# A postnorm attention and FFN layer on one core: the last tile's normed rows turned by VectorE and DMAs instead of TensorE

## The chip, the core and the metric

The kernel runs on one core of a Trainium2 chip. The core has five engines with queues of their own: TensorE (PE in the profile, its weight loads PEld), VectorE (DVE), ScalarE (ACT), GpSimd (POOL) and SyncE (SP, which only issues DMAs here). They share the on-chip memory SBUF; TensorE writes its results to PSUM. The metric is the time of one execution on the device, in microseconds (us).

## What is computed

`x` holds 4 sequences of 512 rows of 1024 numbers, in 32-bit floats. The layer is

```python
q, k, v = x @ w_q.T, x @ w_k.T, x @ w_v.T        # 16 heads of 64
q, k = rope(q), rope(k)
attn = softmax(where(causal, q @ k.T, -1e9) / sqrt(64))
x = layernorm(x + (attn @ v) @ w_out.T)
x = layernorm(x + x @ (weight_int8 * scales[:, None]).T)
```

The second product, the FFN, has an int8 weight of 1024x1024 with one scale for each output.

## The kernel before

**Precision by digits.** TensorE takes its operands in a short float format (`FR`). A 32-bit operand is split into a high digit (ACT rounds a copy) and a low digit (DVE subtracts the high digit from the number), and products are made from digits. In the FFN the weight is int8 and needs one digit, so each FFN product has two parts, `hi` and `lo` (`ffn`, line 667 on). For the products with `w_q`, `w_k`, `w_v` and `w_out` both operands are split in three tiles each, high, low and a difference; those of the weights are `WD[0]` to `WD[2]`, each of 128x1024 numbers.

**Stages.** First come the units of attention (a sequence and a pair of heads each), up to about 740 us. Then come 16 tiles of 128 rows each, `t` from 0 to 15, in one loop, `for t in range(NT_ROWS)`. For a tile there are: the output product of the attention (`out_half`, line 199, two halves of 512 columns with 24 matmuls of 512 columns each), the residual and the first layer norm (`norm`), the turning of the normed rows (`transpose_x1`), the FFN product (`ffn`, line 676, two halves of 16 matmuls), and behind it the scales, the residual and the second norm. `x_sb[t]` is a tile's row buffer through all of this. In the loop the digits of tile `t`'s attention output lie in `WD[t % 3]`.

**Why rows are turned.** TensorE sums over the partitions (the 128 rows of SBUF). The output product leaves a tile with its rows on the partitions, and the FFN needs the 1024 columns there, as 8 blocks of 128. `transpose_x1` has two ways to do that:

- Tiles 0, 1 and 15: eight TensorE transposes of 128x128 into PSUM (line 647), and for each half of the columns a copy by ACT (line 649, the high digit) and a subtraction by DVE (line 650, the low digit).
- Tiles 2 to 14: DVE turns each 32x32 block (line 653, into the one buffer `blocks`), four DMAs on SP's queue carry the four quarters of the partitions to a DRAM tile `turned_x` (line 658), four more bring them back in the wanted order (line 661), into the tile that becomes the low digit. Then ACT copies the high digit (line 664) and DVE subtracts (line 665), in one piece of 128x1024 each. A load of quarter `a` reads what the store of quarter `a` wrote, and each load brings a part of every one of the 8 blocks.

Tiles 0 to 13 and 15 have their digits in the buffers `x1hi` and `x1lo`, of which there is one pair. Tile 14's lie in `WD[1]` (`WD[t % 3]` at `t` = 13), so that its loads need not wait for tile 13's product.

**Order.** TensorE's order is written out by hand (`manual_schedule`). In the loop's last three rounds it is: round 13: first half of tile 15's output product, its second half, (tile 14's turning, which gives TensorE nothing to do), tile 13's FFN product; round 14: tile 15's transposes, tile 14's FFN product; round 15: tile 15's FFN product. The orders on DVE, ACT, SP and POOL are made at build time by a planner, which takes what it reckons ready and prefers what stands earlier in the program; at run time each engine keeps to its order and waits in it. PSUM for the FFN has two buffers of 512 columns (`ps_f`), drained by DVE (lines 684 to 686: times scale, plus residual, statistics). POOL's queue carries the finished tiles to the output, SP's and ACT's queues the two halves of the last one.

Of the kernel before, what the change touches and what calls it, by code (L numbers as in the profile page):

```python
# [16 lines left out]
ALU = mybir.AluOpType  # L17
# [21 lines left out]
def attention_ffn_kernel(  # L39
# [18 lines left out]
    nc = tc.nc  # L58
# [38 lines left out]
    NT_ROWS = B * NI  # L97
# [4 lines left out]
    def norm(r, name, stats=None):  # L102

        if stats is None:
            stats = stp.tile([P, 2, 6], FP, tag="stats", name=f"stats_{name}")
            for n in range(2):
                nc.vector.bn_stats(stats[:, n, :], r[:, ts(n, 512)])
        mean, rstd = moments(name, stats)
        nc.vector.tensor_scalar(r, r, mean, rstd, ALU.subtract, ALU.mult)

    def moments(name, stats):
        mv = stp.tile([P, 2], FP, tag="mv", name=f"mv_{name}")
        nc.vector.bn_aggr(mv, stats)
        rstd = stp.tile([P, 1], FP, tag="rstd", name=f"rstd_{name}")
        nc.scalar.activation(rstd, mv[:, 1:2], AF.Sqrt, bias=eps_sb)
        nc.vector.reciprocal(rstd, rstd)
        return mv[:, 0:1], rstd
# [22 lines left out]
    def digits(name, width):  # L140
        pool = ctx.enter_context(tc.tile_pool(name=name, bufs=1, side=RIGHT_SIDE))
        return [pool.tile([P, NC, width], FR, name=f"{name}_{n}") for n in "hld"]
# [3 lines left out]
    WD = [digits(f"w{k}", P) for k in (2, 1, 0)][::-1]  # L146
# [36 lines left out]
    def load_ao(t, tile=None):  # L183

        tile = staged["w", t % 3] = stage(f"sa_{t}", [P, NC, P]) if tile is None else tile
        nc.sync.dma_start(out=tile, in_=ao[t // NI][:, :, ts(t % NI, P)])

    def load_row(t, queue=nc.sync):
        x_sb[t] = row_tiles[t % 4]
        queue.dma_start(out=x_sb[t], in_=x[ts(t, P), :])  # L190

    def out_product(t, half, n, pool, tag):

        w, r = XD[half], WD[t % 3]
        if n in (0, 2 * NC):
            oprod[n > 0] = pool.tile([P, 512], FP, tag=tag, name=f"y_{t}_{half}_{n}")
        ps = oprod[n >= 2 * NC]
        c, part = (n // 2, n % 2) if n < 2 * NC else (n - 2 * NC, 2)
        nc.tensor.matmul(  # L199
            ps,  # L200
            lhsT=r[part][:, c, :],
            rhs=w[part][:, c, :],
            start=n in (0, 2 * NC),
            stop=n in (2 * NC - 1, NT - 1),
        )
        if n in (2 * NC - 1, NT - 1):
            o = x_sb[t][:, ts(half, 512)]
            nc.vector.scalar_tensor_tensor(o, ps, 1.0 + X12 if n < NT - 1 else -X12, o, op0=MUL, op1=ADD)  # L208
            if half and n == NT - 1:
                norm(x_sb[t], f"a{t}")  # L210

    def high_w(k):
        t = staged["w", k]
        nc.scalar.activation(WD[k][0], t, AF.Copy, scale=LESS)
        nc.scalar.activation(t, t, AF.Copy, scale=1.0 / X12)
# [9 lines left out]
    def split_w(k):  # L225
        low_w(k)
        diff_w(k)
# [399 lines left out]
    with tc.tile_pool(name="row", bufs=1) as rowp, tc.tile_pool(name="sum", bufs=2) as sump, tc.tile_pool(  # L627
        name="ps_x", bufs=2, space=PSUM
    ) as ps_x, tc.tile_pool(name="ps_f", bufs=2, space=PSUM) as ps_f, tc.tile_pool(
        name="ps_o", bufs=2, space=PSUM  # L630
    ) as ps_o:
        x1T = {}

        turned_x = [tc.dram_tile([R, Q, R, NC * Q], FP, name=f"turned_x{n}") for n in range(2)]

        def transpose_x1(t, digits=None):


            if digits is None:
                digits = [rowp.tile([P, NC, P], FR, tag=f"x1{n}", name=f"x1{n}_{t}") for n in ("hi", "lo")]  # L640
            hi, lo = x1T[t] = digits[:2]
            if t in (0, 1, NT_ROWS - 1):

                for n in range(2):
                    ps = ps_x.tile([P, 4, P], FP, tag="xT", name=f"xT_{t}_{n}")
                    for c in range(4):
                        nc.tensor.transpose(ps[:, c, :], x_sb[t][:, ts(4 * n + c, P)], ident)
                    cs = slice(4 * n, 4 * n + 4)
                    nc.scalar.copy(hi[:, cs, :], ps)
                    nc.vector.tensor_tensor(lo[:, cs, :], ps, hi[:, cs, :], ALU.subtract)  # L650
                return
            blocks = rowp.tile([P, R, NC * Q], FP, tag="blocks", name=f"blocks_{t}")
            nc.vector.transpose(
                blocks.rearrange("p r (c s) -> p r c s", s=Q), x_sb[t].rearrange("p (c r s) -> p r c s", r=R, s=Q)
            )
            rows = turned_x[t % 2]
            for a in range(R):
                nc.sync.dma_start(out=rows[:, :, a, :].rearrange("r n w -> n r w"), in_=blocks[ts(a, Q)])
            x1 = lo.bitcast(FP)
            for a in range(R):  # L660
                nc.sync.dma_start(
                    out=x1[:, :, ts(a, Q)], in_=rows[:, :, a, :].rearrange("r n (c s) -> (r n) c s", s=Q)
                )
            nc.scalar.copy(hi, x1)
            nc.vector.tensor_tensor(lo, x1, hi, ALU.subtract)

        def ffn(t, last=False):
            hi, lo = x1T.pop(t)
            r = x_sb.pop(t)
            stats = stp.tile([P, 2, 6], FP, tag="stats", name=f"stats_f{t}")  # L670
            for n in range(2):
                o = ts(n, 512)
                ps = ps_f.tile([P, 512], FP, tag="f", name=f"f_{t}_{n}")
                for c in range(NC):
                    for part in (hi, lo):
                        nc.tensor.matmul(  # L676
                            ps,
                            lhsT=part[:, c, :],
                            rhs=wfv[:, c, o],
                            start=(c == 0 and part is hi),  # L680
                            stop=(c == NC - 1 and part is lo),
                        )
                f = sump.tile([P, 512], FP, tag="sum", name=f"fs_{t}_{n}")
                nc.vector.tensor_mul(f, ps, sc32[:, o])
                nc.vector.tensor_add(r[:, o], f, r[:, o])
                nc.vector.bn_stats(stats[:, n, :], r[:, o])
            if not last:
                norm(r, f"f{t}", stats)
                nc.gpsimd.dma_start(out=out[ts(t, P), :], in_=r)
                return  # L690
            mean, rstd = moments(f"f{t}", stats)
            for n, queue in enumerate((nc.sync, nc.scalar)):
                o = ts(n, 512)
                nc.vector.tensor_scalar(r[:, o], r[:, o], mean, rstd, ALU.subtract, ALU.mult)
                queue.dma_start(out=out[ts(t, P), o], in_=r[:, o])

        def out_half(t, half):
            for n in range(NT):
                out_product(t, half, n, *((pjp, "pj") if half else (ps_o, "o")))

        with tc.manual_schedule(engines={mybir.EngineType.PE}):
            for t in range(NT_ROWS):
                early = t + 2
                if 1 < t < NT_ROWS - 2:
                    out_half(early, 0)
                if t + 3 < NT_ROWS:
                    if t:
                        load_row(t + 3)
                    load_ao(t + 3, raw_ao)
                    high_w(t % 3)  # L710
                    split_w(t % 3)
                if t == 0:
                    out_half(1, 1)
                    transpose_x1(0)
                    out_half(2, 1)
                    out_half(3, 0)
                elif early < NT_ROWS:
                    transpose_x1(t)
                    out_half(early, 1)
                if t == NT_ROWS - 3:  # L720

                    transpose_x1(t + 1, WD[t % 3])
                if t == NT_ROWS - 2:
                    transpose_x1(t + 1)
                ffn(t, t == NT_ROWS - 1)


# [44 lines left out]
```

## Time and profile before

| | us |
|---|---|
| median of 3 runs (lowest to highest) | 1020.71 (1020.62 to 1022.29) |
| profiled execution | 1022.38 |
| its span, first to last instruction | 1020.6 |
| mean granted clock of TensorE | 0.995 of full |

| engine | busy us | share | instructions |
|---|---|---|---|
| PE (matmul) | 1000.3 | 98% | 4628 |
| PEld (weight load) | 744.0 | 73% | 4628 |
| DVE | 853.1 | 84% | 1246 |
| ACT | 388.3 | 38% | 841 |
| POOL | 204.1 | 20% | 283 |

The profile is of one execution. Its times are counted from the first instruction. A row of a timeline gives start, length, engine, line of the program, operation, output `<-` inputs with their shapes, how many, and in brackets the idle time of that engine ahead of it and what ended that. A row of the chain of waits gives start, length and the work that the end of the run was waiting for in that stretch. SPq, DVEq and the like are the queue of an engine issuing or waiting, not computing. "us to landing" of a DMA runs from its issue to the arrival of its data. Tiles appear under the names of their buffers: the row buffers are `row`, `cos_sb` and `sin_sb`, and digits that lie in a weight's place are `w_h` and `w_l`.

### The profile page before, as it was taken

Reading aid. Unit: us, or ns where it says so; the run is one execution under the profiler, and the core shown is the slowest. Engines: PE = TensorE matmul, PEld = TensorE weight load, DVE = VectorE, ACT = ScalarE, POOL = GpSimd, SP = SyncE. Lnnn points to the kernel's source line nnn. Section 1 sums busy time; section 2 is a strip of 40 time slices with the busy share of each in tenths; the row PEclk is TensorE's granted clock in tenths of the full one; section 3 lists DMA queues with packets and bytes.
Section 4 is the critical chain, followed back from the end, with each engine's and each line's share of the span. In section 5 each row is a group of like instructions: output and inputs, shape, how many; then the busy total and the mean of one; then the engine's idle time right before and its main releaser. Section 6 shows DMA issues by size and latency. Waiting matters only on the chain.

```text
span 1020.6 us, 13749 instructions
## 1 busy us (share of the span) xinstructions
PE 1000.3 (98%) x4628; PEld 744.0 (73%) x4628; DVE 853.1 (84%) x1246; ACT 388.3 (38%) x841; POOL 204.1 (20%) x283
## 2 busy tenths in 40 slices
PE   9999999999999999999999999998899999999997
PEld 4667777777777667777777777775588888888885
DVE  5998888888888999788898888888898877878776
ACT  4524444354544435445344453444332122121110
POOL 0122332222322322332223322231300000000000
PEclk9999999999999999999999999999999999999999
DMA  7576676867768786676867758688645465563541
GB/s 288 168 234 210 212 233 190 263 210 217 223 196 262 249 244 225 195 253 190 253 218 201 247 175 270 215 252 275 206 135 154 124 160 145 125 169 103 144 104 62
DMA packets 264022, 204.09 MB, mean 200 GB/s; under 512 B 147600, under 2 KB 220304, under 8 KB 263824
## 3 DMA queue, kind: packets, MB, share of 16 engines
q1 hardware_dynamic: 256176, 184.60, 60.4%
q10 hardware_dynamic: 5616, 10.75, 2.8%
q0 software_dynamic: 2160, 7.87, 1.9%
q8 instruction: 37, 0.61, 0.3%
q14 instruction: 33, 0.27, 0.1%
HBM read 112.46 MB, written 73.92 MB: 183 GB/s over the span
## 4 chain that ended last, share of the span: by engine, by line
PE 88%; DVE 5%; issue 3%; DMA 2%; ACT 1%; POOL 1%; SPq 0%; ACTq 0%; DVEq 0%; POOLq 0%
PE p L276 44%; PE y L199 17%; PE f L676 11%; PE s L409 7%; PE o L490 6%; PE pw L261 3%; DVE pr L463 1%; DVE x_d L177 1%; POOL pr L458 1%; DVE x_l L173 1%; DVE nmx L430 0%; DMA rot<-raw 0%; DVE raw L318 0%; DMA sx<-in_xT 0%; DVE w_l L219 0%
## 5 line engine op out<-in xcount | busy, mean ns | idle before, releaser
L458 POOL TENSOR_SCALAR pr<-pr,rden 128x128 f32<-128x128 f32 (+3 forms) x256 | 192.9, 772 | 528.6 <-DVE rden L452 464.7
L276 PE MATMUL p<-x_h,w_h 128*128 128x512 f32 x736 | 290.2, 394 | 0.0
L276 PE MATMUL p<-x_l,w_l 128*128 128x512 f32 x736 | 286.8, 390 | 0.0
L276 PE MATMUL p<-x_d,w_d 128*128 128x512 f32 x736 | 190.9, 395 | 2.8 <-DVE v L318 2.4
L444 ACT ACTIVATE pr<-s,nmx 128x128 f32<-128x128 f32 (+3 forms) x256 | 131.4, 531 | 115.5 <-DVE nmx L430 110.2
L276 PEld LDWEIGHTS p<-x_h,w_h 128*128 128x128 f32 x736 | 138.1, 188 | 50.4 <-issue 22.0
L276 PEld LDWEIGHTS p<-x_d,w_d 128*128 128x128 f32 x736 | 135.5, 188 | 36.1 <-issue 5.1
L276 PEld LDWEIGHTS p<-x_l,w_l 128*128 128x128 f32 x736 | 138.2, 188 | 28.1
L295 ACT ACTIVATE tA<-p 128x512 f32<-128x512 f32 x92 | 55.1, 599 | 223.4 <-PE p L276 218.4
L463 DVE STREAM_TRANSPOSE pr<-pr 128x768 f32<-128x768 f32 (+1 forms) x96 | 99.6, 1056 | 24.4 <-POOL pr L458 22.5
L199 PE MATMUL y<-x_h,w_h 128*128 128x512 f32 x256 | 101.7, 397 | 4.4 <-ACT tA L295 3.9
L430 DVE TENSOR_REDUCE nmx<-s 128x2 f32<-128x256 f32 (+3 forms) x128 | 102.0, 820 | 4.2 <-PE s L419 1.1
L199 PE MATMUL y<-x_l,w_l 128*128 128x512 f32 x256 | 101.4, 396 | 2.2 <-DVE x_l L173 2.1
L676 PE MATMUL f<-wf,x1hi 128*128 128x512 f32 x240 | 93.4, 389 | 0.0
L676 PE MATMUL f<-wf,x1lo 128*128 128x512 f32 x240 | 93.4, 389 | 0.0
L409 PE MATMUL s<-qk 64*128 64x384 f32 (+3 forms) x512 | 80.2, 446 | 1.0 <-DVE qk L242 1.0
L490 PE MATMUL o<-prT,va 128*64 128x256 f32 (+3 forms) x512 | 76.0, 439 | 0.5 <-ACT pr L444 0.5
L223 DVE TENSOR_TENSOR w_d<-w_h,w_l 128x1024 fp32r<-128x1024 f32 x60 | 74.5, 1241 | 1.5
L318 DVE SCALAR_TENSOR_TENSOR raw<-p,tA 128x512 f32<-128x512 f32 x61 | 41.8, 685 | 38.4 <-PE p L276 38.4
L490 PEld LDWEIGHTS o<-prT,va 128*64 128x64 f32 x512 | 33.9, 136 | 46.2 <-issue 40.0
L199 PE MATMUL y<-x_d,w_d 128*128 128x512 f32 x256 | 64.9, 396 | 0.5 <-DVE sin_sb L208 0.5
L199 PEld LDWEIGHTS y<-x_h,w_h 128*128 128x128 f32 x256 | 48.6, 190 | 15.7 <-ACT tA L295 4.3
(112 smaller groups left out, 1157.4 us busy)
## 6 DMA issues: line engine op xcount, KB each, us to landing
turned<-pr SPq DMA_DIRECT2D x64, 384.0 KB, 3.6
rot<-raw SPq DMA_DIRECT2D x128, 128.0 KB, 2.7
turned<-pr SPq DMA_DIRECT2D x32, 512.0 KB, 4.5
prT<-turned SPq DMA_DIRECT2D x32, 512.0 KB, 5.3
prT<-turned SPq DMA_DIRECT2D x32, 384.0 KB, 4.0
turned_v<-v SPq DMA_DIRECT2D x32, 256.0 KB, 4.7
va<-turned_v SPq DMA_DIRECT2D x128, 64.0 KB, 2.8
prT<-turned SPq DMA_DIRECT2D x32, 256.0 KB, 3.3
```

What stands on the lines that cost most here:

```text
L199: nc.tensor.matmul(ps, lhsT=r[part][:, c, :], rhs=w[part][:, c, :], start=n in (0, 2 * NC), stop=n in (2 * NC - 1, NT - 1),)
L223: nc.vector.tensor_tensor(d, h, l, SUB)
L276: nc.tensor.matmul(ps, lhsT=w[part][:, c, :], rhs=r[part][:, c, :], start=n in (0, 2 * NC), stop=n in (2 * NC - 1, NT - 1),)
L295: nc.scalar.activation(prod["tA"], ps, AF.Copy, scale=1.0 + X12)
L318: nc.vector.scalar_tensor_tensor(raw_tile(u, k), ps, -X12, prod["tA"], op0=MUL, op1=ADD)
L409: nc.tensor.matmul(ps[:, j, at : at + n], lhsT=t[rows, 0, ts(i, P)], rhs=keys[rows, :, : (i + 1) * Q], start=True, stop=u not in BUSY,)
L430: nc.vector.tensor_reduce(nmx[:, 2 * i : 2 * i + 2], ps[:, :, at : at + n], AX.X, ALU.max, negate=True)
L444: nc.scalar.activation(pr[:, :, at // P : at // P + i + 1, j, :], ps[:, j, at : at + n].rearrange("p (r k s) -> p r k s", r=R, s=Q), AF.Ex ...
L458: nc.gpsimd.tensor_scalar(p, p, rden[:, m : m + 1], 1.0, ALU.mult, ALU.mult)
L463: nc.vector.transpose(t, t)
L490: nc.tensor.matmul(ps[j * D : (j + 1) * D, kb * P :], lhsT=v[:, kb, 2 * j : 2 * j + 2, :].rearrange("p a s -> p (a s)"), rhs=t[:, :, 4 * k ...
L676: nc.tensor.matmul(ps, lhsT=part[:, c, :], rhs=wfv[:, c, o], start=(c == 0 and part is hi), stop=(c == NC - 1 and part is lo),)
```

## The change

Tile 15 no longer takes the way over TensorE. It is turned as tiles 2 to 14 are, and its `transpose_x1` moves from round 14 into round 13, behind tile 14's and ahead of tile 13's FFN product. Its digits lie in `WD[(13 + 1) % 3]`, that is `WD[2]`, where tile 14's attention output was. For this tile alone copy and subtraction are made in two halves of four column blocks each; all other tiles keep one piece.

```diff
-            if t in (0, 1, NT_ROWS - 1):
+            if t < 2:
...
-            nc.scalar.copy(hi, x1)
-            nc.vector.tensor_tensor(lo, x1, hi, ALU.subtract)
+            for cs in (slice(0, 4), slice(4, 8)) if t == NT_ROWS - 1 else (slice(0, 8),):
+                nc.scalar.copy(hi[:, cs, :], x1[:, cs, :])
+                nc.vector.tensor_tensor(lo[:, cs, :], x1[:, cs, :], hi[:, cs, :], ALU.subtract)
...
                 if t == NT_ROWS - 3:
 
                     transpose_x1(t + 1, WD[t % 3])
-                if t == NT_ROWS - 2:
-                    transpose_x1(t + 1)
+                    transpose_x1(t + 2, WD[(t + 1) % 3])
                 ffn(t, t == NT_ROWS - 1)
```

## The prediction

> **What bounds the kernel now.** I read the page first (TensorE, PE, busy 98% of the span), then the chain of waits over the last 120 us, then each engine's timeline over the last 45 us, then the landing times of the two DMA lines. All times below are us on the axis of the kernel before. The chain:
>
> ```profile
> 979.24 10.92 PE y L199 x48
> 990.16 7.27 PE f L676 x32
> 997.43 0.87 PE xT L647 x8
> 998.30 14.75 PE f L676 x64
> ...
> 1016.00 0.03 issue
> 1016.02 0.55 DVE row L694
> 1016.57 0.46 DVEq L768
> ```
>
> From 900 to 1013 the path is PE alone, without a gap. The eight transposes of the last tile (xT, L647) lie on it, between the second product of tile 13 and that of tile 14. Behind 1013 stands a tail of VectorE (DVE), a square root and the last DMA, which the change does not touch. So PE work taken away here shortens the run one for one, as long as PE is given no wait in its place. The exact starts:
>
> ```profile
> 997.26 1.04 PE L647 MATMUL xT<-ident,row 128*128 128x128 f32 x8
> 998.05 0.48 PE L676 MATMUL f<-wf,w_h 128*128 128x512 f32 x1
> 998.37 0.40 PE L676 MATMUL f<-wf,w_l 128*128 128x512 f32 x1
> ```
>
> The transposes hold PE from 997.26 to 998.05, 0.79. The first product after them stands 0.32 before its follower, others 0.23. The two products of 32 matmuls on both sides, one window each (length, then PE and weight-load busy time with counts, granted clock, DMA share, GB/s):
>
> ```profile
> 990.00:997.26 7.26, 7.26 (x32) 5.82 (x31) 1.00 0.00 0
> 998.05:1005.61 7.56, 7.55 (x33) 6.11 (x33) 1.00 0.18 69
> ```
>
> Tile 14's product takes 0.30 longer than tile 13's at the same granted clock, 1.00.
>
> **What the change removes: PE's transposes.** Surely 0.79. With them goes the stretched first product, 0.32 - 0.23 = 0.09. The other 0.21 of the 0.30 runs through all of tile 14's product. It may be an after-effect of the transposes (then it goes) or belong to digits that lie in a weight's buffers (then it stays, and tile 15's product, now fed from such buffers too, gains up to 0.30 as well). So PE's saving lies between 0.79 - 0.30 = 0.49 and 0.79 + 0.30 = 1.09. The nearest row speaks against the buffers: the products of line 199 read such buffers as weights, and 16 of them from 984.56 to 988.18 are 0.226 apart. I take 0.79 + 0.09 + half of 0.21 = 1.0. Tile 15's product, at 1005.61 before, could then start at 1004.6 (1004.8 if only the 0.79 is gained).
>
> Also removed are two ACT copies (L649) and two DVE subtractions (L650) out of PSUM. Their successors have the same number and width (128x512), so on these engines they are moved, not saved.
>
> **What it adds: a trip for the last tile.** It is one 128x1024 DVE block transpose (L653), four DMAs to DRAM (L658) and four back (L661) on SP's queue, then copy and subtraction in halves. DVE around the place:
>
> ```profile
> 974.23 0.81 DVE L109 TENSOR_SCALAR row<-row,mv_a,rstd_a 128x1024 f32<-128x1024 f32 x1
> 975.08 1.25 DVE L653 STREAM_TRANSPOSE blocks<-row 128x1024 f32<-128x1024 f32 x1
> 976.25 0.65 DVE L684 TENSOR_TENSOR fs<-f,sc 128x512 f32<-128x512 f32 x1
> ...
> 993.19 0.81 DVE L109 TENSOR_SCALAR row<-row,mv_a,rstd_a 128x1024 f32<-128x1024 f32 x1
> 993.92 0.68 DVE L684 TENSOR_TENSOR fs<-f,sc 128x512 f32<-128x512 f32 x1
> ...
> 997.46 0.69 DVE L684 TENSOR_TENSOR fs<-f,sc 128x512 f32<-128x512 f32 x1 [1.41 <-PE f L676]
> ```
>
> Tile 14's block transpose followed its norm after 0.85 and stood ahead of the product's drain (L684). The code puts tile 15's likewise ahead of tile 13's product, so it should start at 993.19 + 0.85 and end at F = 995.3. It pushes tile 13's first drain back by 1.17, and the 1.41 of idle time before 997.46 hides that; without this cover, DVE would be 1.17 late to the second drain, done with that PSUM buffer by 999.3, and PE wants it for tile 14's second half at 1000.9.
>
> SP's queue and the landings (first line 658, out; then line 661, in):
>
> ```profile
> 976.35 0.95 SPq L658 DMA_DIRECT2D turned_x<-blocks  x2
> 979.27 2.61 SPq L661 DMA_DIRECT2D x1lo<-turned_x  x4
> 981.92 1.43 SPq L658 DMA_DIRECT2D turned_x<-blocks  x2
> 983.40 4.16 SPq L661 DMA_DIRECT2D w_l<-turned_x  x4
> 1016.60 0.36 SPq L695 DMA_DIRECT2D out<-row  x1
> ...
> DMA to landing us min/median/max: 2.0/3.0/4.7
> ...
> DMA to landing us min/median/max: 3.1/3.5/4.6
> ```
>
> After tile 14's loads SP issues nothing until 1016.6, so nothing is queued behind the eight new issues and their waits except the final store, 12 us later. The steps:
>
> - Out: the first issue is at F, the other three about 0.48 apart (0.95 for two), so the last is at F + 1.5. By the median landing of 3.0 the last lies in DRAM at F + 4.5.
> - In: each load waits for the store of its own quarter only. The last goes at F + 4.5 and lands at F + 8.0 by the median of 3.5. Counted the other way, from the first load at F + 2.1 and tile 13's row (first issue 979.27, copy started 984.81, 5.5), it is F + 7.6. I take F + 7.8 = 1003.1.
> - Bounds: all minima give F + 1.5 + 2.0 + 3.1 = 1001.9; all maxima F + 1.5 + 4.7 + 4.6 = 1006.1.
> - Halves: ACT copies one in 0.54 (1.08 for two), done at 1003.65; DVE subtracts in 0.65, done at 1004.3. The second halves end at about 1004.2 and 1004.95.
> - Needed: the first half's high digit at 1004.6, its low digit 0.23 later, at 1004.85; the second half 1.8 after the start, at 1006.4. So PE waits for nothing, with some 0.5 to spare. Undivided, copy and subtraction (1.05 and 1.23) would end at 1005.4 and cost about 0.5; the halves take that away.
>
> Is DVE free then? Tile 13's last scaling ended by 1002.1, with the two old subtractions ahead of it; without them by 1000.9. Tile 14's first drain takes 2.2 from 1001.1. From 1003.3 until tile 14's second drain at about 1004.8 DVE is idle, and the two new subtractions (1.3) fit almost exactly; they push that drain back by at most 0.2. What is late next would be tile 15's second drain, before which DVE idles 1.44 now, so the tail keeps its length. GpSimd's queue (POOL) only stores finished rows; tile 13's store (512 KB, 4.9 to landing) moves from 1002.46 to about 1001.3 and may meet the last loads. Tile 14's loads, which met such a store, took 4.5 at the median, tile 13's 3.4: 1.1 later, landing 1004.2 and a wait of 0.55. The buffers cost nothing: that weight's last use, tile 14's output product, ended by 972.
>
> [...]
>
> [...]
>
> **Sum.** -1.0 with no wait. Against the profiled execution, 1022.38 (span 1020.6 and 1.8 around it), that is 1021.4; this execution lies 1.7 above the median of the runs shown, 1020.71, which becomes 1019.7. The runs fall into two places, 1020.6 to 1020.7 and 1022.3 to 1022.4, so a median of the changed kernel may land on the upper one by itself.
>
> **Rivals.**
>
> - *A short wait.* The trip is late by more than the 0.5 to spare: the meeting with the store (0.55) gives 1019.7 + 0.55 = 1020.3; all maxima give 1006.1 + 0.55 + 0.65 - 1004.85 = 2.45 and 1022.15. If DVE took tile 13's first drain before the block transpose, F would move by 2.2 and the wait would be 1.7: 1021.4. For it: small slack on a chain of eight transfers. Against it: SP and the DMA engines are empty from 990 to 1002.
> - *DVE's order turns against it (slower).* The order on DVE and ACT is made by a planner that guesses landings. If it puts the low digits behind tile 14's second drain, which can't start before 1004.8, they come at 1004.8 + 2.2 + 0.65 = 1007.65, a wait of 2.8: 1022.5. Behind that tile's moments and scaling too (1005.81 to 1009.49 now, 3.7) they come at 1009.15: a wait of 4.3, 1024.0. It decides from a wait of 3.0 on. For it: the margin is 1.5. Against it: tile 13's subtraction stood where DVE idled 0.44 for it and tile 14's where it idled not at all, so the guesses are close, and err early.
> - *The transposes' time is not saved.* Tile 14's product might not be able to start earlier. Its digits are ready at 993.1, 4 us ahead, and its PSUM buffer is drained by 996; excluded but for the first rival.
>
> **Numbers.** No wait 0.57; short wait, up to 3.0, 0.28; DVE's or ACT's order or a longer trip, 0.12; a gain over 2.0 us, for which no row gives a ground, 0.03. About 0.2% (2.04 us) is what a measurement of this kernel tells from no change, so the first two are both "within": 0.85. The predicted time is that of no wait with a trace of the store's meeting, 1019.8. Its own range is 1019.4 (saving 1.09 and 0.2 of scatter) to 1020.3. To hold 8 in 10 the range goes up through the short waits and the upper place of the runs, to 1021.9; below, to 1019.3.
>
> **What would show it.** Right: no xT from tile 15 on PE, tile 15's block transpose ending near 995.3, eight DMAs on SP between 995.3 and 1000, the copy's first half starting near 1003.1, and the two tile products following each other without a gap, the chain being PE until 1012. If the saving is 1.0, tile 14's product takes some 7.4. Wrong: idle time on PE before tile 15's product, named as ACT's copy or DVE's subtraction; or the block transpose behind tile 13's drain; or both late products at 7.56, which would put the slow pace on the buffers.

## The result, and the profile after

| | median us | lowest to highest | runs |
|---|---|---|---|
| before | 1022.25 | 1020.62 to 1022.68 | 6 |
| changed | 1025.70 | 1024.57 to 1029.28 | 6 |

The ratio is 1.0039, with a 95% interval of 1.0026 to 1.0053: about 4 us slower. The forecast was 1019.8, in a range of 1019.3 to 1021.9, with a chance of 0.12 for slower. It was wrong.

Single runs of one kernel differ by 2 to 5 us, as much as the effect. In the profiles these differences lie ahead of the place of the change, from about 700 us on (last section). So the kernels are compared below also over one stretch of their profiles: from the first matmul of tile 13's FFN product to the first instruction of the last drain. It takes 23.08 us before (990.00 to 1013.07) and 26.96 in the changed kernel (991.50 to 1018.46). The difference, 3.88, lies within that of the whole runs (2.7 to 5.4 us). What follows the stretch takes 7.5 us in all kernels here.

The chain of waits of the changed kernel over this stretch (start, length, what the end was waiting for):

```profile
980.74 10.92 PE y L199 x48
991.66 14.75 PE f L677 x64
1006.40 0.02 issue
1006.43 0.70 DVE fs L685
1007.13 0.02 issue
1007.15 0.70 DVE row L686
1007.86 0.02 issue
1007.88 0.70 DVE stats_f L687
1008.58 0.02 issue
1008.61 0.07 DVE mv_f L113
...
1008.81 0.70 DVE w_l L666
1009.52 0.04 issue
1009.56 8.88 PE f L677 x31
```

The transposes are gone, and the products of tiles 13 and 14 stand as one piece of 64. Then the chain leaves PE, where before it did not leave it at all. For 3.1 us it runs through VectorE: tile 14's second drain (fs, row, stats_f), the joining of its statistics (mv_f), and only then tile 15's low digit (w_l). On PE that is:

```profile
1006.00 0.39 PE L677 MATMUL f<-wf,w_l 128*128 128x512 f32 x1
1006.23 0.40 PE L677 MATMUL f<-wf,w_h 128*128 128x512 f32 x1
1009.56 0.80 PE L677 MATMUL f<-wf,w_l 128*128 128x512 f32 x1 [2.94 <-DVE w_l L666]
1010.15 0.63 PE L677 MATMUL f<-wf,w_h 128*128 128x512 f32 x1
```

Tile 15's first matmul, on the high digit, runs at once, and its second waits for the low digit. The matmuls behind the wait are slow as well, 0.4 to 0.6 apart instead of 0.23. The windows of the two products and of the gap between (length; busy time and count of PE, PEld, DVE, ACT and POOL; granted clock; DMA share; GB/s) show why:

```profile
998.76:1006.23 7.47, 7.47 (x34) 6.02 (x32) 5.31 (x9) 1.44 (x3) 0.53 (x1) 1.00 0.83 194
1006.23:1009.56 3.33, 0.40 (x2) 0.00 (x1) 3.03 (x6) 0.29 (x1) 0.00 (x0) 0.94 0.00 0
1009.56:1018.46 8.90, 8.86 (x31) 6.79 (x31) 3.51 (x7) 0.00 (x0) 0.53 (x1) 0.83 0.16 61
```

The granted clock falls at the end of the gap, to a mean of 0.94 over it, and of 0.83 over the rest of tile 15's product. Read as stretches at half clock, that is 2 x 0.06 x 3.33 + 2 x 0.17 x 8.90 = 3.4 us. Shorter windows (same columns) show the half clock itself and its end:

```profile
1009.50:1011.50 2.00, 1.94 (x5) 1.56 (x6) 1.49 (x4) 0.00 (x0) 0.18 (x1) 0.50 0.04 8
1011.50:1013.50 2.00, 2.00 (x8) 1.63 (x7) 0.00 (x0) 0.00 (x0) 0.35 (x1) 0.73 0.56 215
1013.50:1015.50 2.00, 2.00 (x11) 1.58 (x10) 0.74 (x2) 0.00 (x0) 0.00 (x0) 1.00 0.12 47
```

The trip itself was nearly on time. The block transpose, behind one instruction of tile 13's drain (L685), then SP's queue, then ACT's copies:

```profile
995.42 0.69 DVE L685 TENSOR_TENSOR fs<-f,sc 128x512 f32<-128x512 f32 x1
996.02 1.24 DVE L653 STREAM_TRANSPOSE blocks<-row 128x1024 f32<-128x1024 f32 x1
```

```profile
997.29 1.78 SPq L658 DMA_DIRECT2D turned_x<-blocks  x4
999.34 2.71 SPq L661 DMA_DIRECT2D w_l<-turned_x  x4
1021.98 0.36 SPq L696 DMA_DIRECT2D out<-row  x1
```

```profile
1001.39 0.30 ACT L115 ACTIVATE rstd_f<-mv_f,eps_sb 128x1 f32<-128x1 f32 x1 [7.70 <-DVE mv_f L113]
1004.82 1.14 ACT L665 CAST w_h<-w_l 128x512 fp32r<-128x512 f32 x2 [3.13 <-DMA w_l<-turned_x]
```

The copies began 13.3 us after tile 13's first matmul, where the prediction had 13.1. The first high digit was ready at about 1005.4, 0.8 ahead of TensorE's use of it. VectorE stood idle then, and its next instruction in order was not the low digit:

```profile
1004.14 0.69 DVE L687 BATCH_NORM_STATS2 stats_f<-row 128x6 f32<-128x512 f32 x1
1006.43 0.69 DVE L685 TENSOR_TENSOR fs<-f,sc 128x512 f32<-128x512 f32 x1 [1.59 <-PE f L677]
...
1008.61 0.21 DVE L113 BATCH_NORM_AGGREGATE mv_f<-stats_f 128x2 f32<-128x12 f32 x1
1008.81 1.29 DVE L666 TENSOR_TENSOR w_l<-w_l,w_h 128x512 fp32r<-128x512 f32 x2
1010.02 0.16 DVE L116 RECIPROCAL rstd_f<-rstd_f 128x1 f32<-128x1 f32 x1
```

From 1004.8 to 1006.4 VectorE waits for TensorE to end tile 14's product, while the subtraction that TensorE needs next, ready from 1005.4 on, is queued behind that wait.

### The profile page after: what moved, and what is told of

Same layout as the page of the kernel before. It is cut to its first block, busy times and chain, and to the rows that moved or that the text cites. A ratio compares the mean times of both kernels' runs of the same rounds, so it can differ in the third digit from the quotient of the medians.

```text
span 1026.0 us, 13752 instructions
## 1 busy us (share of the span) xinstructions
PE 1001.9 (98%) x4620; PEld 744.9 (73%) x4620; DVE 854.5 (83%) x1247; ACT 388.6 (38%) x841; POOL 204.1 (20%) x283
## 4 chain that ended last, share of the span: by engine, by line
PE 87%; DVE 5%; DMA 3%; issue 3%; POOL 1%; SPq 0%; ACT 0%; ACTq 0%; DVEq 0%; POOLq 0%
PE p L276 43%; PE y L199 17%; PE f L677 12%; PE s L409 7%; PE o L490 6%; PE pw L261 2%; POOL pr L458 1%; DMA sx<-in_xT 1%; DVE pr L463 1%; DMA rot<-raw 1%; DMA turned<-pr 1%; DMA raw_x<-in_xT 1%; DVE x_l L173 1%; DVE x_d L177 1%; DVE w_l L219 0%
## 5 line engine op out<-in xcount | busy, mean ns | idle before, releaser
L677 PE MATMUL f<-wf,x1hi 128*128 128x512 f32 x224 | 87.2, 389 | 0.0
L677 PE MATMUL f<-wf,x1lo 128*128 128x512 f32 x224 | 87.2, 389 | 0.0
```

The source lines that it names most:

```text
L677: nc.tensor.matmul(ps, lhsT=part[:, c, :], rhs=wfv[:, c, o], start=(c == 0 and part is hi), stop=(c == NC - 1 and part is lo),)
```

## The experiments

Theory A: the place of the low digits in VectorE's order makes the wait. Theory B: the trip through DRAM is too long. Theory C, beside A: the idle time makes the clock drop, and that is the rest of the loss. Each expectation below was written before its kernel ran. e7_no_trip and e4_whole have one execution each, so for them only the stretch is compared. All segments are read from the profiles, in us; "second" is tile 15's second matmul, the first that needs a low digit.

| kernel | 13 to 14 | 14 to 15 | 15 to second | second to drain | stretch |
|---|---|---|---|---|---|
| before | 8.06 | 7.55 | 0.23 | 7.24 | 23.08 |
| changed | 7.26 | 7.47 | 3.33 | 8.90 | 26.96 |
| e1_order | 7.26 | 7.47 | 0.24 | 7.43 | 22.40 |
| e2_order2 | 7.26 | 7.47 | 0.24 | 7.43 | 22.39 |
| e3_busy | 7.26 | 10.67 | 0.23 | 7.43 | 25.60 |
| e5_whole | 7.26 | 7.47 | 1.05 | 7.53 | 23.31 |
| e7_no_trip | 7.26 | 7.47 | 3.20 | 8.96 | 26.89 |
| e4_whole | 7.26 | 7.46 | 3.86 | 10.05 | 28.64 |
| e6_place | 7.27 | 7.47 | 0.24 | 7.43 | 22.40 |
| e8_before_place | 8.06 | 7.55 | 0.23 | 7.23 | 23.08 |

### The order alone

```diff
-                nc.vector.tensor_tensor(lo[:, cs, :], x1[:, cs, :], hi[:, cs, :], ALU.subtract)
+                low_digit[t] = nc.vector.tensor_tensor(lo[:, cs, :], x1[:, cs, :], hi[:, cs, :], ALU.subtract)
...
-                nc.vector.tensor_mul(f, ps, sc32[:, o])
+                drain = nc.vector.tensor_mul(f, ps, sc32[:, o])
+                if (t, n) == (NT_ROWS - 2, 1):
+                    queue_after(drain, low_digit[t + 1])
```

`queue_after` tells the planner only that the drain comes later in VectorE's order; no wait is added or taken away. In the two profiles the orders on TensorE, ScalarE and GpSimd are the same, and that on VectorE differs in the place of these two subtractions alone.

> The changed kernel with one thing added: on VectorE the two low digits of tile 15 are queued ahead of tile 14's second drain, instead of behind it and its statistics. Nothing else on any engine moves. Theory A (VectorE's order makes the wait): the copies were done at 1005.4 and 1006.0 in the changed kernel's profile, so the low digits come at about 1006.1 and 1006.7; TensorE wants the first at 1006.5. It does not wait, its clock stays full, and from tile 13's first product to the last drain it is 7.27 + 7.47 + 7.6 = 22.35 us, against 23.07 before and 26.96 in the changed kernel: 0.7 us faster than before. Theory B (the trip through DRAM lands too late): the wait stays near 3 us and the time at 3 to 4 us above before.

VectorE in this kernel:

```profile
1002.89 0.70 DVE L693 BATCH_NORM_STATS2 stats_f<-row 128x6 f32<-128x512 f32 x1
1004.19 1.30 DVE L666 TENSOR_TENSOR w_l<-w_l,w_h 128x512 fp32r<-128x512 f32 x2 [0.61 <-ACT w_h L665]
1005.40 0.69 DVE L689 TENSOR_TENSOR fs<-f,sc 128x512 f32<-128x512 f32 x1
```

and the windows of its three products:

```profile
990.24:997.50 7.26, 7.26 (x33) 6.00 (x32) 6.72 (x10) 1.12 (x2) 0.00 (x0) 1.00 0.08 17
997.50:1004.97 7.47, 7.47 (x34) 6.02 (x32) 6.09 (x11) 1.44 (x3) 0.53 (x1) 1.00 0.83 194
1004.97:1012.63 7.66, 7.62 (x33) 5.83 (x31) 5.67 (x10) 0.30 (x1) 0.53 (x1) 1.00 0.18 71
```

The two subtractions now start as soon as the first copy is done, the drain follows 0.2 us later than TensorE would allow, and the clock stays at 1.00. The stretch is 22.40 where 22.35 was expected: 4.56 less than in the changed kernel, with the same trip, copies and halves. In whole runs this kernel's ratio to the one before is 1.0001 (0.9990 to 1.0012), median 1022.39 against 1021.67. The loss of the changed kernel is gone, but the 0.7 us gained in the stretch does not show in whole runs (last section).

### The block transpose too

The same rule once more: `queue_after(drain, block_turn[t + 2])` at tile 13's first drain.

> The first experiment's order, and also tile 15's block transpose queued ahead of tile 13's first drain, as the prediction had it; in the changed kernel one instruction of that drain went first and the transpose ended 0.6 us later. Theory A: the whole trip moves 0.6 earlier, its end is off the path already, so the time is that of the first experiment within 0.2 us. If the first experiment still shows a short wait ahead of tile 15, it is gone here and the time is lower by that much, at most 0.6 us.

The block transpose ended 5.29 after tile 13's first matmul, where the prediction had 5.3 and the changed kernel 5.76, and the copies started 0.45 earlier. The stretch stayed, 22.39. The ratio was 1.0003 (0.9994 to 1.0012). So that delay, also an effect of VectorE's order, cost nothing.

### Without the trip

```diff
+            if t == NT_ROWS - 1:
+                x1 = x_sb[t].rearrange("p (c s) -> p c s", s=P)
+                for cs in (slice(0, 4), slice(4, 8)):
+                    nc.scalar.copy(hi[:, cs, :], x1[:, cs, :])
+                    tail.append((lo[:, cs, :], x1[:, cs, :], hi[:, cs, :]))
+                return
             blocks = rowp.tile([P, R, NC * Q], FP, tag="blocks", name=f"blocks_{t}")
```

In `ffn` of tile 14 the subtractions of `tail` are queued right behind the joining of the statistics.

> The changed kernel with tile 15's trip left out: no block transpose and no DMAs for it, its digits are made from the rows unturned, so the product of this tile is of other numbers. ACT's copies then end some 8 us earlier. The two low digits are queued on VectorE where the changed kernel has them, right behind tile 14's last statistics. Theory A (the place in VectorE's order alone makes the wait): the low digit still comes at about 18 us after tile 13's first product, tile 15's second matmul waits 3.1 us, the clock halves, and the stretch is 26.5 to 27.0 as in the changed kernel (26.96). Theory B (the trip's length matters): without the trip the wait falls to near nothing and the stretch to about 22.4.

ACT and then PE of this kernel:

```profile
992.65 1.14 ACT L655 CAST w_h<-row 128x512 fp32r<-128x512 f32 x2 [1.85 <-DVE row L109]
```

```profile
1003.34 0.40 PE L687 MATMUL f<-wf,w_h 128*128 128x512 f32 x1
1006.54 0.79 PE L687 MATMUL f<-wf,w_l 128*128 128x512 f32 x1 [2.80 <-DVE w_l L702]
```

The high digits were ready 9 us ahead, there was no trip, and the wait (2.96 against 3.10) and the stretch (26.89 against 26.96) are nearly those of the changed kernel. With the first experiment this settles A against B: with the trip and another order there is no wait, without the trip and with the same order there is all but 0.14 of it.

### TensorE kept busy in the gap

```diff
+                if t == NT_ROWS - 1:
+                    busy = ps_x.tile([P, 512], FP, tag="xT", name="busy")
+                    for n in range(14):
+                        nc.tensor.matmul(busy, lhsT=wfv[:, 0, :P], rhs=wfv[:, 0, :512], start=True, stop=True)
                 ffn(t, t == NT_ROWS - 1)
```

> The changed kernel with 14 further 512-column matmuls on TensorE between the products of tiles 14 and 15, about 3.2 us of work on a buffer that nobody reads. VectorE's order stays as in the changed kernel, so tile 15's low digit still comes at the same time. Theory C (the idle 2.9 us make the granted clock drop to half for 3.4 us, which costs some 1.6 us behind the wait): TensorE is not idle, the clock stays 1.00 in tile 15's product, and the time falls by 1.4 to 1.7 us against the changed kernel, to about 2.3 us above before. If the slow matmuls at the start of tile 15's product come from its buffers or from the second half of the digits arriving late, the time stays or rises by up to 0.3.

```profile
996.56:1004.02 7.46, 7.46 (x33) 6.01 (x32) 5.31 (x9) 1.44 (x3) 0.53 (x1) 1.00 0.84 194
1004.02:1007.22 3.20, 3.20 (x15) 2.63 (x14) 2.90 (x6) 0.29 (x1) 0.00 (x0) 1.00 0.02 5
1007.22:1014.89 7.67, 7.63 (x33) 5.75 (x31) 3.65 (x8) 0.00 (x0) 0.53 (x1) 1.00 0.17 68
```

These are tile 14's product, the added matmuls and tile 15's product. Useless work of 3.20 us in the gap leaves the clock at 1.00, and the rest of tile 15's product takes 7.43 instead of 8.90. So the drop of the clock is worth 1.47 us of the stretch, and the stretch falls by 1.36. In whole runs the fall does not show: median 1025.86 of 4 runs, ratio to before 1.0039 (1.0026 to 1.0052), the same as the changed kernel's, where the stretch alone would give 1.0025. The place within the stretch is shown, the gain in the total is not.

### The halves

Copy and subtraction in one piece, with the corrected order, and then with the changed kernel's order:

```diff
-            for cs in (slice(0, 4), slice(4, 8)) if t == NT_ROWS - 1 else (slice(0, 8),):
+            for cs in (slice(0, 8),):
```

> The first experiment's order on VectorE, but copy and subtraction of tile 15 in one piece of 1024 columns. From the rows of the changed kernel: copy from 1004.8 to 1005.9, subtraction to 1007.15, wanted at 1006.5: a wait of 0.65 us on TensorE and 0.65 us more than the first experiment, with the clock still full. If the halves are worth nothing, the time equals the first experiment's.

With the corrected order the wait is 1.05 - 0.24 = 0.8, a little over the 0.65 expected, and the stretch 0.91 longer. After a wait of this length the rest of the product takes 7.53, close to the 7.43 without a wait and far from the 8.90 of the changed kernel. In whole runs the ratio to before is 1.0017 (1.0008 to 1.0026), more than the 1.0002 that the stretch would give.

> The changed kernel without the halves: copy and subtraction of tile 15 in one piece, VectorE's order otherwise the changed kernel's (the low digits behind tile 14's last statistics). Theory A: the subtraction starts where it does now, about 17.3 us after tile 13's first product, and takes 1.23 instead of 0.69, so the wait grows by 0.55 and the stretch from 26.96 to about 27.5. If the copies' end decided, the wait would grow by more, or the halves would have no effect.

With the changed kernel's order the wait grew by 0.53, as expected. The stretch grew by 1.68, three times the forecast. The windows of tile 14's product, the gap and the rest of tile 15's product say where that went:

```profile
996.27:1003.74 7.47, 7.47 (x34) 5.95 (x32) 5.31 (x9) 1.35 (x2) 0.53 (x1) 1.00 0.84 194
1003.74:1007.60 3.86, 0.40 (x2) 0.07 (x1) 3.56 (x6) 0.29 (x1) 0.00 (x0) 0.84 0.00 0
1007.60:1017.65 10.05, 10.02 (x31) 7.65 (x31) 2.91 (x5) 0.00 (x0) 0.53 (x1) 0.72 0.14 54
```

Half clock lasted 2 x 0.16 x 3.86 + 2 x 0.28 x 10.05 = 6.9 us by these rounded means, twice the 3.4 of the changed kernel. The drop comes in portions (last section).

### The slow pace of the late products

The last open term was the 0.21 us by which tile 14's product is slow throughout. Two kernels move digits out of the weights' buffers. The first (e6_place) has e2_order2's order and the edit below; its expectation calls e2_order2 the third experiment. The second (e8_before_place) is the kernel before, with tile 14's digits moved alone.

```diff
-                    transpose_x1(t + 1, WD[t % 3])
-                    transpose_x1(t + 2, WD[(t + 1) % 3])
+                    transpose_x1(t + 1, [d[:, :, :P] for d in XD[0]])
+                    transpose_x1(t + 2, [d[:, :, P : 2 * P] for d in XD[0]])
```

> The order of the third experiment's kernel (block transpose and low digits of tile 15 ahead of the drains), and the digits of tiles 14 and 15 moved from the weights' buffers into the first 256 columns of the high and low digits of w_out's first half, which are free by then. Nothing else changes. If the slow pace of the two late products (7.47 and 7.66 us, 0.233 a matmul, against 7.26 and 0.227 for tile 13) belongs to the weights' buffers, both fall to about 7.26 and 7.46, and the stretch from tile 13's first product to the last drain falls from 22.39 to about 22.0. If it belongs to the place in the program or to what the other engines do then, it stays at 22.4.

> The kernel before, with TensorE's transposes of tile 15 in their place, but tile 14's digits moved from the weight's buffers into the first 128 columns of w_out's first half. If the weights' buffers make tile 14's product slow, it falls from 7.55 to about 7.35 (only the first matmul behind the transposes stays stretched) and the time by 0.2 us; if the transposes make it slow, it stays at 7.55.

Nothing moved: 7.47 and 7.67 in the first, 7.55 in the second. The whole runs agree: 0.9998 (0.9985 to 1.0012) and 0.9998 (0.9984 to 1.0013). So it is not the weights' buffers as such. The transposes are not the cause either, since tile 14's product is just as slow where there are none. Nor is it that one product directly follows another: before, tile 15's product follows tile 14's, and its matmuls are 0.227 apart on average. In the last three products of all ten profiles, matmuls on digits in `x1hi` and `x1lo` are 0.227 apart; those on digits in the weights' buffers or in `w_out`'s are 0.233 apart, leaving aside the first after the transposes and those behind a wait. No run put tile 14's digits into `x1hi` and `x1lo`, so what sets the pace stays open; it is worth 0.2 us for each product.

## Why the prediction was wrong

- **PE's saving: right in kind, 0.3 too large.** The 0.79 of the transposes came out as 0.80. The stretched first matmul (0.09) went too. "Half of 0.21" was a mis-sized term: none of it went, and tile 15's product took on the slow pace as well, 7.43 instead of 7.24 behind its first matmul, 0.19 more. The saving was 0.7, not 1.0, inside the bounds of 0.49 to 1.09. Both late products being slow is what the prediction's other branch, digits in a weight's buffers, forecast; but moving the digits to `w_out`'s buffers changed nothing, so the reason stays open.
- **The trip: right, with two misses that partly cancel.** Counted from tile 13's first matmul, F (the block transpose's end) was forecast at 5.3 and came at 5.76, because one instruction of tile 13's drain went ahead. From there to the copies' start it took 7.6, where 7.8 was forecast: the stores landed in 2.3 at the median instead of 3.0, the loads in 3.4 instead of 3.5. So the copies' start, forecast at 13.1, came at 13.3. GpSimd's store did not hurt the trip: it was issued at 1003.02, and the loads, the last issued at 1001.3, landed in 3.7 at most.
- **"Is DVE free then?": the step that failed.** The text found VectorE idle in time (1003.3 to 1004.8 on its axis) and concluded that "the two new subtractions (1.3) fit almost exactly"; the sum stood on that, "with no wait". The measured wait was 3.10. VectorE's 1.59 us of idle time ahead of tile 14's second drain were of no use to the subtractions, which stood behind that drain in its order. The planner, whose order is fixed before the run, had put the subtractions behind tile 14's second drain and the joining of its statistics; the first experiment and the one without the trip show that this order alone makes the wait of 3.1.
- **The rival that named it was given 0.12 and too low a price.** Its two places were behind the drain (wait 2.8) and behind the scaling (4.3); the real one lies between (3.1). The evidence held against it, that two earlier subtractions had been queued well, was weak: two places in an order do not show what the planner takes a landing to be. The margin of 1.5 was the idle time before the drain; by the prediction's own times the first copy's end (1003.65) left 1.15 to the drain (1004.8), and the changed kernel had about 1 (copy done at 1005.4, drain possible at 1006.4). What the planner reckoned is not in the profile; that it came out on the other side of the drain is.
- **The clock was missing from the price.** "It decides from a wait of 3.0 on" took a wait at its own length. A wait of 3.1 cost 3.1 + 1.47. The sum closes: -0.80 - 0.08 + 3.10 + 1.47 + 0.19 = 3.88. The kernel before had shown such drops itself, ahead of the place of the change (first fence of the last section).
- **The halves: right in kind, too small.** Forecast to be worth about 0.5 with the order as assumed, they were worth 0.9.

## What to carry to other kernels

When work moves to an engine whose order is made by a planner, read where the new instruction stands in that order and what the one ahead of it waits for; idle time in the old timeline does not show it. Fixing the order of two subtractions turned a loss of 3.9 us into a gain of 0.7 over the stretch (whole runs show the loss gone, but no gain), so a change like this is to be judged with its order written out. And a wait of 3.1 us on TensorE cost 1.47 more than its length here, because the clock dropped.

## What the runs showed of the hardware

**Idle time and the clock.** In the changed kernel tile 15's second matmul came 3.1 us late (2.9 of idle time), and the clock was at half for 3.4 us. Without the trip it came 3.0 late (2.8 of idle time), and the rest of the product took 8.96, as long as the changed kernel's 8.90. In e4_whole it came 3.6 late, and the clock was at half for 6.9 us. In e5_whole it came 0.8 late, and the rest of the product took 7.53, close to the 7.43 without a wait. In the changed kernel's trace the granted clock falls to half at 701.97, 736.10 and 1009.17 and comes back at 708.79, 739.51 and 1012.58: every distance between these times is, within 0.01 us, a multiple of 3.4133 us (34.13 is 10 of them, 307.20 is 90). So these changes keep one beat, from 700 to 1013 us. At the drop at 1009.17 TensorE had been idle for 2.5 us, since 1006.6.

So the clock fell to half with 2.5 us of idle time behind it, in a wait whose idle time was 2.9 us in all, and a wait of 0.8 us left the pace nearly as it was. No run here shows what a wait between 0.8 and 3.0 us does to the clock.

**The spread of the runs.** The kernel before, from 700 to 712 and from 732 to 742 us, where attention gives way to the row tiles:

```profile
700.00:712.00 12.00, 9.50 (x40) 6.69 (x40) 9.90 (x13) 3.67 (x4) 0.00 (x0) 0.86 1.03 355
732.00:742.00 10.00, 7.93 (x33) 5.23 (x33) 7.45 (x10) 3.67 (x5) 0.00 (x0) 0.83 0.35 113
```

the changed kernel:

```profile
700.00:712.00 12.00, 9.17 (x32) 6.96 (x32) 10.02 (x12) 3.66 (x4) 0.00 (x0) 0.72 1.01 342
732.00:742.00 10.00, 7.91 (x32) 5.05 (x32) 7.44 (x10) 3.40 (x3) 0.00 (x0) 0.83 0.46 134
```

and the second experiment:

```profile
700.00:712.00 12.00, 8.88 (x38) 6.50 (x38) 9.81 (x12) 3.66 (x4) 0.00 (x0) 0.86 1.01 345
732.00:742.00 10.00, 7.91 (x40) 5.10 (x40) 8.95 (x12) 4.17 (x5) 0.00 (x0) 1.00 0.38 116
```

The instructions of each engine are the same there and in the same order, and the number of portions at half clock is not: two, three and one. Tile 13's product starts at 990.00, 991.50 and 989.02 in these three, so a portion goes with 1 to 1.5 us. Of the ten profiles, five have one portion (starts from 988.6 to 989.3), two have two (990.0 and 990.2) and two have three (991.3 and 991.5). The tenth has two in one place and starts at 993.4, for a reason that stays open. The whole runs bear this out. In the 29 runs of the kernel before that stand beside the first experiments, the mean time is 1021.10 us at a granted clock of 0.997 (11 runs), 1021.36 at 0.996 (4), 1022.76 at 0.995 (7), 1023.09 at 0.994 (5) and 1025.07 at 0.993 (2). A straight line through the 29 spans gives 0.84 us for each 0.001 of the clock. One portion is 0.0017 of it (half of 3.41 over 1020), which makes 1.4 us a portion. That the portions cause the spread, and do not only go with it, is likely but not shown.

It is also the likely reason why whole runs do not show the 0.7 us. By their ratios, e1_order, e2_order2, e3_busy and e5_whole are 0.8 to 1.5 us longer than their stretch accounts for, and their mean clock is 0.9940 to 0.9948 against 0.9956 before, though the rest of tile 15's product, 7.43 to 7.53 us in their four profiles, shows no drop of the clock within the stretch. Why their clock was lower stays open.
